# Fewer steps per layer norm, another division of the last tile's attention units, and a later shared expert in a two-layer decoder kernel

## The chip, the core and the metric

The kernel runs on one core of a Trainium2 chip. The core has a matrix engine (TensorE, PE in the profile, with its weight loads as PEld), a vector engine (VectorE, DVE), a scalar and activation engine (ScalarE, ACT), a general engine (GpSimd, POOL) that here mostly issues indirect DMAs, and a queue engine (SyncE, SP) that issues the other DMAs. Each engine works through its own list of instructions in order; semaphores make one wait for another. The metric is device time in microseconds from the start of the program to its end, lower is better; of several runs the median counts.

## The reference

Two decoder layers work on 4 sequences of 256 tokens, 256 wide. Cut to what is computed:

```python
x = x + linear_attention(layernorm(x))   # 16 heads, decayed running sums of k*v and k
x = x + experts_by_token_id(layernorm(x))  # 4 experts, weights taken from ctx
x = x + product_key_memory(layernorm(x)) # 8 heads, 8 of 45*45 rows each, gathered from a table
x = x + local_attention(layernorm(x))    # causal convolution, then blocks of 16 tokens
x = x + cross_attention(layernorm(x), ctx)  # 16 heads of 16, each token against 1024 keys
x = x + moe(layernorm(x))                # shared SwiGLU + 2 of 16 routed SwiGLU experts

def layernorm(x, eps=1e-05):
    m, v = mean(x), var(x)
    return (x - m) / sqrt(v + eps)
```

In the cross attention queries, keys and values are rounded to 8-bit steps, and so are the softmax weights: each row is scaled so that its largest entry is 255 and rounded to whole numbers. The last block is `shared_output + routed_output`, with the two gates divided by their sum.

## The kernel before

**Tiles.** The 1024 tokens lie in NT = 8 tiles of 128 rows; `xt[t]` is tile t's residual in SBUF. A batch is two tiles. The first three blocks run by batch in `front(b)`, the others by tile.

**Order.** TensorE, ScalarE and VectorE get their instructions in an order that the kernel makes itself. Every piece of work is a Python generator that yields the engine it needs next and, if it has to, a condition. `Clock` keeps an estimate of when each engine is free (`note`), and `weave` always advances the generator that could begin first, less its `lead`, then by `rank`. The estimates exist only while the program is built; what remains is a fixed order on each engine. So an instruction more or less in one generator can move all others after it. `fork` starts several generators and waits for them all. PSUM is given out in banks (`Banks.take`, `give`); from `turn` on there are two pairs and three single ones.

**Stages.** `front(b)` norms, projects with w_qkv, scans, norms, runs the four experts, norms, raises with w_up, lowers with w_down, projects with w_q, compares with keys, and `choose` finds the best rows on VectorE; its result is `idxT`. `fetches` then has POOL gather the rows: 64 chunks of eight indirect DMAs, three buffers `g`, so that a chunk is fetched only when the third before it was summed. `weigh` multiplies and reduces a chunk on VectorE (`g`, `z`, `u`), takes tanh on ScalarE, fills `blk` and sums on TensorE into `accs`. When tile t has all eight chunks, `local_attention(t)` and `queries(t)` follow, then 16 `units`, one per head.

**A unit** takes a pair of banks, makes scores for 1024 keys on TensorE (`psc`), their maximum on VectorE (`mx`), a bias from it on ScalarE (`nb`), the exponentials as uint8 on ScalarE (`e`), four bytes at a time transposed on TensorE, cast from uint8 to bf16 on ScalarE (`qqT`), and multiplied by the values on TensorE into `accs[:, 1]`. At most two units may be between transposition and sum. Three streams share all 128 units: stream k takes units k, k + 3 and so on.

**After the units.** `cross_out` divides, projects and adds. `routes` runs `route` for tiles (0,1), (2,3), (4,5), (6), (7): norm (its rows are stored to `xs` in DRAM), gate logits, two best experts, counts in `took` and `prior`, ranks. After tile 7 it forks `maps` (slots for all rows: `rmap` and `smap`), `gates` and `shared`; for the other tiles `gates` and `shared` follow one another. `shared` is the shared expert: `ph` from w_s13, tanh, `hd`, transposition, `py` from w_s2a and w_s2b, addition to `xt`. The expert loop (`up`, `down`, from line 1344) is outside `weave`: POOL gathers 128 rows by `smap`, TensorE transposes them (`tpx`), multiplies by the expert's weights, and POOL scatters the results by `rmap`. Its PSUM pool takes over the banks.

**The layer norm** computes a reciprocal root on VectorE, without a table: a first guess from the bits of the variance, then three Newton steps of three instructions each on a [128, n] tile (`layernorm_T`, from line 329).

Of the kernel before, what the change touches and what calls it, by code (L numbers as in the profile page):

```python
# [11 lines left out]
F32 = mybir.dt.float32  # L12
BF16 = mybir.dt.bfloat16
I32 = mybir.dt.int32
# [7 lines left out]
P = 128  # L22
# [182 lines left out]
def decoder(ctx, tc, a, out):  # L205
# [123 lines left out]
    def layernorm_T(pool, sfx, tiles, dst, col0=0, store=None):  # L329

        n = len(tiles)
        mv = pool.tile([P, n, 2], F32, name="ln_mv", tag="ln_mv" + sfx)
        for i, t in enumerate(tiles):
            st = pool.tile([P, 6], F32, name="ln_st", tag="ln_st" + sfx, bufs=2)
            ve_.bn_stats(st, xt[t])
            yield "vector", None
            ve_.bn_aggr(mv[:, i, :], st)
            yield "vector", None

        ve = pool.tile([P, n], F32, name="ln_ve", tag="ln_ve" + sfx)  # L340
        ve_.tensor_scalar(ve, mv[:, :, 1], EPS, None, ALU.add)
        yield "vector", None
        half = pool.tile([P, n], I32, name="ln_half", tag="ln_half" + sfx)
        ve_.tensor_scalar(half, ve.bitcast(I32), 1, None, ALU.logical_shift_right)
        yield "vector", None
        rstd = pool.tile([P, n], F32, name="ln_rstd", tag="ln_rstd" + sfx)
        ve_.tensor_scalar(rstd.bitcast(I32), half, -1.0, float(0x5F3759DF), ALU.mult, ALU.add)
        yield "vector", None
        nt = pool.tile([P, n], F32, name="ln_nt", tag="ln_nt" + sfx)
        for _ in range(3):  # L350
            ve_.scalar_tensor_tensor(nt, rstd, -0.5, rstd, ALU.mult, ALU.mult)
            yield "vector", None
            ve_.tensor_tensor(nt, nt, ve, ALU.mult)
            yield "vector", None
            ve_.scalar_tensor_tensor(rstd, nt, 1.5, rstd, ALU.add, ALU.mult)
            yield "vector", None
        nmr = pool.tile([P, n], F32, name="ln_nmr", tag="ln_nmr" + sfx)
        ve_.scalar_tensor_tensor(nmr, mv[:, :, 0], -1.0, rstd, ALU.mult, ALU.mult)
        yield "scalar", None
        xns = []  # L360
        for i, t in enumerate(tiles):
            xn = pool.tile([P, D], F32, name="ln_xn", tag="xnTq" if sfx == "q" else "ln_xn" + sfx,
                           bufs=1 if sfx in "lq" else 2)
            se_.activation(xn, xt[t], AF.Identity, scale=rstd[:, i:i + 1], bias=nmr[:, i:i + 1])
# [12 lines left out]
        yield "vector", None  # L377
# [673 lines left out]

    weighted = [0]

    def units(k, n):

        work = A.work
        for j in range(k, NT * XH, n):
            t, h = j // XH, j % XH
            yield "tensor", lambda: qready.get(t)
            o, c = h % 2, h // 2  # L1060
            hr = slice(o * 64, o * 64 + 64)
            psc = yield from bank.take([P, T], n=2)
            for n_ in range(2):
                te_.matmul(psc[:, n_ * 512:(n_ + 1) * 512], QT[t][hr, c, :], kT[hr, c, n_ * 512:(n_ + 1) * 512],
                           start=True, stop=True)
            yield "vector", None
            mx = work.tile([P, 1], F32, name="mx", tag="mx", bufs=4)
            ve_.tensor_reduce(mx, psc, AX.X, ALU.max)
            yield "scalar", None
            nb = work.tile([P, 1], F32, name="nb", tag="nb", bufs=4)  # L1070
            se_.activation(nb, mx, AF.Identity, scale=NSQ[t][:, h:h + 1], bias=ln255)

            e = work.tile([P, T], U8, name="e", tag="e", bufs=3)
            se_.activation(e, psc, AF.Exp, bias=nb, scale=SQ[t][:, h:h + 1], accum_out=SUMS[t][:, h:h + 1])
# [68 lines left out]
    def route(*tiles):  # L1143
        work = A.work2
        n, t0 = len(tiles), tiles[0]
        xnT = work.tile([P, 2, n * P], F32, name="xnT6", tag="xnT6")
        yield from layernorm_T(work, "r", tiles, xnT, store=xs)
        pl = yield from bank.take([P, n, NE])
        for i in range(n):
# [25 lines left out]
        se_.copy(rank[:, t0:t0 + n, :], prk)  # L1175
        bank.give(prk)
        if t0 + n == NT:
            yield from ck.fork(maps(), gates(tiles, sg), shared(tiles, xnT), ahead=(4.0, 0.0, 0.0))
        else:
            yield from gates(tiles, sg)  # L1180
            yield from shared(tiles, xnT)

    def gates(tiles, sg):
        work, n, t0 = A.work2, len(tiles), tiles[0]
# [7 lines left out]
        ve_.reciprocal(ws, ws)  # L1192
        ve_.tensor_tensor(gs, gs, ws.to_broadcast([P, n, 2]), ALU.mult)

    def shared(tiles, xnT):
        work, n = A.work2, len(tiles)
        yield "tensor", None

        hds = []
        for i, t in enumerate(tiles):  # L1200
            ph = yield from bank.take([P, 2, EI])
            for k in range(2):
                te_.matmul(ph.rearrange("p j n -> p (j n)"), xnT[:, k, i * P:(i + 1) * P], A.s13[:, k, :],
                           start=(k == 0), stop=(k == 1))
            yield "scalar", None
# [26 lines left out]
        bank.give(py)  # L1232
        yield "vector", None

    def maps():

        work, keep = A.work2, A.w2
        yield "tensor", None
        pcn = yield from bank.take([P, NE])
        te_.matmul(pcn, ones, prior[:, NT, :], start=True, stop=True)  # L1240
# [32 lines left out]
        for t0 in (0, NT):  # L1273
# [11 lines left out]
        ve_.tensor_tensor(past, bc(iotat, 2, NE), bc(last, 1, NSL), ALU.is_ge)  # L1285
        tef = work.tile([P, NSL], F32, name="tef", tag="tef")
        ve_.tensor_reduce(tef, past, AX.X, ALU.add)
        A.te = keep.tile([P, NSL], I32, name="te", tag="te")
        ve_.tensor_scalar(A.te, tef, float(NE - 1), None, ALU.min)
# [6 lines left out]
        bank.give(pmap)  # L1296
        A.smap = keep.tile([P, NSL], I32, name="smap", tag="smap")
        ve_.tensor_scalar(A.smap, A.rmap, 1, T - 1, ALU.logical_shift_right, ALU.bitwise_and)

        se_.activation(part0[:, 0:1], part0[:, 0:1], AF.Silu)  # L1300
        none = work.tile([P, NSL], F32, name="none", tag="none")
# [25 lines left out]
    with tc.manual_schedule(engines={mybir.EngineType.PE, mybir.EngineType.Activation, mybir.EngineType.DVE}):  # L1327

        ck.weave([*[Stream(follow(b), (3.0, 0.0, 0.0, 0.0)[b], (0.0, 20.0, 0.0, 0.0)[b], (0, 0, 1, 1)[b]) for b in range(NB)],
                  Stream(keys_values(), 0.0, 25.0, 1), Stream(fetches(), 20.0), Stream(weigh(), rank=0), Stream(turn()), Stream(free()),  # L1330
                  Stream(weights()), Stream(locals_()), Stream(all_queries(), rank=0), *[Stream(after_turn(units, k, 3)) for k in range(3)],
                  Stream(cross_out()), Stream(routes())])
    w13, w2a, w2b = A.w13, A.w2a, A.w2b
    work_ctx.close()
# [142 lines left out]
```

## Time and profile before

| what | value |
|---|---|
| runs | 1258.58, 1258.76, 1255.35 us; median 1258.58 |
| the profiled execution | 1113.02 us |
| its span, first to last instruction | 1111.3 us |
| mean granted TensorE clock in it | 0.752 of full speed |
| batch 0's front, up to the first gather | 0 to 111.7 us |
| gathers on POOL | 111.7 to 845.9 us, 512 of them |
| copy of tile 7's queries (qT) done | 929.6 us |
| last sum of tile 7's units | 982.0 us |
| first gather of the expert loop | 1004.7 us |
| first transposition of the expert loop | 1010.5 us |

The profiled execution took 1.7 us more than its span. It was 145.6 us shorter than the median of the runs. The profile is of one execution; its instruction times are those of that execution. A row of the timeline gives start, duration, engine, line, operation, output and inputs, shape and number of instructions merged, and in brackets how long the engine had been idle and who released it. Line 77 is the helper through which all woven instructions are recorded, so they are told apart by the names of their tiles.

### The profile page before, as it was taken

Reading aid. Unit: us, or ns where it says so; the run is one execution under the profiler, and the core shown is the slowest. Engines: PE = TensorE matmul, PEld = TensorE weight load, DVE = VectorE, ACT = ScalarE, POOL = GpSimd, SP = SyncE. Lnnn points to the kernel's source line nnn. Section 1 sums busy time; section 2 is a strip of 40 time slices with the busy share of each in tenths; the row PEclk is TensorE's granted clock in tenths of the full one; section 3 lists DMA queues with packets and bytes.
Section 4 is the critical chain, followed back from the end, with each engine's and each line's share of the span. In section 5 each row is a group of like instructions: output and inputs, shape, how many; then the busy total and the mean of one; then the engine's idle time right before and its main releaser. Section 6 shows DMA issues by size and latency. Waiting matters only on the chain. (4 is left out here: it accounts for less than half of the span.)

```text
span 1111.3 us, 15428 instructions
## 1 busy us (share of the span) xinstructions
PE 803.7 (72%) x4945; PEld 494.9 (45%) x4945; DVE 785.0 (71%) x2312; ACT 560.9 (50%) x1168; POOL 572.4 (52%) x597
## 2 busy tenths in 40 slices
PE   4772578926862887766887888878887777838993
PEld 3561455613650665333544554344543443314551
DVE  5459877688779768997778777788867676543233
ACT  2231232511421254655787767787767798832221
POOL 3000766575777577767777667776663000003551
PEclk9786678966985898665868686588956777556997
DMA  6001565586677578759876667767662600001223
GB/s 226 1 4 40 145 196 152 154 246 163 188 194 194 150 198 233 201 165 270 231 205 185 180 176 193 192 188 199 173 192 86 208 11 1 5 5 50 79 81 133
DMA packets 65710, 163.75 MB, mean 147 GB/s; under 512 B 14890, under 2 KB 28571, under 8 KB 65628
## 3 DMA queue, kind: packets, MB, share of 16 engines
q0 software_dynamic: 35072, 106.99, 33.9%
q1 hardware_dynamic: 29404, 54.18, 18.2%
q10 hardware_dynamic: 1152, 1.57, 0.4%
q8 instruction: 40, 0.66, 0.2%
q14 instruction: 42, 0.34, 0.1%
HBM read 156.93 MB, written 5.77 MB: 146 GB/s over the span
## 5 line engine op out<-in xcount | busy, mean ns | idle before, releaser
L77 POOL DMA_INDIRECT g<-in_table,idxT x512 | 517.2, 1010 | 319.4 <-issue 147.0
L77 DVE TENSOR_REDUCE mx<-bank 128x1 f32<-128x1024 f32 x128 | 155.1, 1217 | 60.7 <-PE bank L77 54.2
L77 ACT ACTIVATE e<-bank,nb,qs_q 128x1024 uint8<-128x1024 f32 x128 | 154.0, 1203 | 4.3
L77 PE MATMUL accs<-g,blk 128*32 128x256 f32 x1024 | 99.2, 523 | 71.4 <-DVE blk L77 64.6
L77 ACT CAST qqT<-bank 128x1024 bf16<-128x1024 uint8 x128 | 126.8, 1009 | 21.6 <-PE bank L77 20.8
L1349 POOL DMA_INDIRECT xr<-xs,smap x24 | 23.3, 969 | 183.0 <-DVE none L77 158.8
L77 PE MATMUL bank<-kT,qT 64*128 64x512 bf16 x256 | 98.3, 496 | 21.6 <-ACT e L77 19.6
L77 DVE TENSOR_TENSOR g<-g,hb 128x1024 f32<-128x1024 f32 x64 | 78.1, 1221 | 14.7 <-DMA g<-in_table,idxT 10.1
L77 PE MATMUL bank<-ident,e 128*128 128x128 f32 x256 | 68.2, 371 | 26.0 <-ACT e L77 19.5
L77 PEld LDWEIGHTS accs<-g,blk 128*32 128x32 f32 x1024 | 33.0, 136 | 119.2 <-DVE blk L77 76.9
L77 DVE TENSOR_REDUCE z<-g 128x8 f32<-128x1024 f32 x64 | 78.1, 1220 | 2.2
L77 ACT ACTIVATE nb<-mx,ln,nsq 128x1 f32<-128x1 f32 x128 | 49.6, 388 | 44.6 <-DVE mx L77 44.4
L77 PEld LDWEIGHTS <-qqT 128*128 128x128 bf16 x1024 | 38.4, 102 | 68.5 <-ACT qqT L77 49.2
L77 PEld LDWEIGHTS bank<-ident,e 128*128 128x128 f32 x256 | 34.1, 177 | 77.6 <-ACT e L77 35.1
L77 PE MATMUL accs<-vi,qqT 128*128 128x16 bf16 x1024 | 46.8, 174 | 22.4 <-ACT qqT L77 22.1
L77 ACT ACTIVATE th<-u 128x16 f32<-128x16 f32 x64 | 13.9, 218 | 96.1 <-DVE u L77 90.0
L77 ACT ACTIVATE ln_xn<-x,ln_nmr,ln_rstd 128x256 f32<-128x256 f32 x48 | 27.2, 595 | 39.4 <-DVE ln_nmr L77 37.9
L77 PE MATMUL bank<-ident,ln_xn 128*128 128x128 f32 x96 | 23.3, 354 | 32.6 <-ACT ln_xn L77 17.7
L1358 PE MATMUL ph<-w,xrT 128*128 x96 | 37.6, 512 | 5.0 <-DVE xrT L1355 5.0
L1362 DVE TENSOR_TENSOR hd<-hd,ph 128x176 f32<-128x176 f32 x24 | 8.1, 338 | 43.8 <-ACT hd L1361 43.8
L77 PE MATMUL bank<-w_ctxT,aT 128*128 128x256 f32 x128 | 32.8, 407 | 3.9 <-DVE aT L77 2.6
L77 PE MATMUL bank<-ident,ix 128*128 128x128 f32 x8 | 3.5, 439 | 42.8 <-DVE ix L77 42.8
(293 smaller groups left out, 1673.1 us busy)
## 6 DMA issues: line engine op xcount, KB each, us to landing
hb<-hdram SPq DMA_DIRECT2D x128, 256.0 KB
g<-in_table,idxT POOLq DMA_INDIRECT x512
w<-in_w SPq DMA_DIRECT2D x16, 352.0 KB
w_w2a<-in_w SPq DMA_DIRECT2D x1, 2048.0 KB
x<-in_x SPq DMA_DIRECT2D x8, 128.0 KB
w_ctxT<-in_ctxT SPq DMA_DIRECT2D x1, 1024.0 KB
w_w_up<-in_w_up SPq DMA_DIRECT2D x1, 1024.0 KB
xs<-ln_xn SPq DMA_DIRECT2D x8, 128.0 KB
```

What stands on the lines that cost most here:

```text
L77: return emit(*args, **kw)
L1349: nc.gpsimd.indirect_dma_start(out=xr, out_offset=None, in_=xs, in_offset=bass.IndirectOffsetOnAxis(ap=smap[:, i:i + 1], axis=0))
L1358: nc.tensor.matmul(ph.rearrange("p j n -> p (j n)"), xrT[:, k, :], w13[:, bass.ds(e, 1), k, :], start=(k == 0), stop=(k == 1))
L1362: nc.vector.tensor_tensor(hd, hd, ph[:, 1, :], ALU.mult)
```

## The change

It has four parts.

1. *Layer norm.* The three Newton steps become one third-order step (four instructions) and one Newton step (three), with a constant factor moved between them.
2. *Last tile's units.* `units` gets a range. Tiles 0 to 6 keep three streams, tile 7 has four of its own. For tile 7 `nb` is made by VectorE for all heads, and `qqT` by VectorE for odd heads.
3. *Shared experts.* Tile 6's `shared` no longer follows its `gates`: it becomes a stream of its own with a lead 2.0 smaller, which starts when tile 7's units are summed. Tile 7's waits for it, but its first product `ph`, and the counts `pcn` of `maps`, are put on TensorE before the fork. Tile 6 and tile 7 get their own `xnT6` buffers (the tag names tile 6 apart from the rest).
4. *Maps.* `rmap` and `smap` are computed before `past`, `tef` and `te` instead of after them; `past` takes the buffer of `cols`.

```diff
@@ layernorm_T
-        for _ in range(3):
-            ve_.scalar_tensor_tensor(nt, rstd, -0.5, rstd, ALU.mult, ALU.mult)
-            yield "vector", None
-            ve_.tensor_tensor(nt, nt, ve, ALU.mult)
-            yield "vector", None
-            ve_.scalar_tensor_tensor(rstd, nt, 1.5, rstd, ALU.add, ALU.mult)
-            yield "vector", None
+        ve_.tensor_tensor(nt, rstd, rstd, ALU.mult)
+        yield "vector", None
+        ve_.tensor_tensor(nt, nt, ve, ALU.mult)
+        yield "vector", None
+        ve_.scalar_tensor_tensor(nt, nt, -10.0 / 3.0, nt, ALU.add, ALU.mult)
+        yield "vector", None
+        ve_.scalar_tensor_tensor(rstd, nt, 5.0, rstd, ALU.add, ALU.mult)
+        yield "vector", None
+        ve_.scalar_tensor_tensor(nt, rstd, -0.5 * 0.375 ** 3, rstd, ALU.mult, ALU.mult)
+        yield "vector", None
+        ve_.tensor_tensor(nt, nt, ve, ALU.mult)
+        yield "vector", None
+        ve_.scalar_tensor_tensor(rstd, nt, 1.5 * 0.375, rstd, ALU.add, ALU.mult)
+        yield "vector", None
@@ units
-    def units(k, n):
+    def units(lo, hi, k, n):
-        for j in range(k, NT * XH, n):
+        for j in range(lo + k, hi, n):
...
-            yield "scalar", None
             nb = work.tile([P, 1], F32, name="nb", tag="nb", bufs=4)
-            se_.activation(nb, mx, AF.Identity, scale=NSQ[t][:, h:h + 1], bias=ln255)
+            if t < NT - 1:
+                yield "scalar", None
+                se_.activation(nb, mx, AF.Identity, scale=NSQ[t][:, h:h + 1], bias=ln255)
+            else:
+                ve_.tensor_scalar(nb, mx, NSQ[t][:, h:h + 1], ln255, ALU.mult, ALU.add)
+                yield "scalar", None
...
-            yield "scalar", None
+            late = t == NT - 1 and h % 2 == 1
+            yield "vector" if late else "scalar", None
             qqT = work.tile([P, 8, P], BF16, name="qqT", tag="qqT", bufs=2)
-            se_.copy(qqT.rearrange("p (o j) q -> p o j q", o=2), tp.bitcast(U8).rearrange("p o (q j) -> p o j q", j=4))
+            (ve_.tensor_copy if late else se_.copy)(qqT.rearrange("p (o j) q -> p o j q", o=2),
+                                                    tp.bitcast(U8).rearrange("p o (q j) -> p o j q", j=4))
@@ route
-        xnT = work.tile([P, 2, n * P], F32, name="xnT6", tag="xnT6")
+        xnT = work.tile([P, 2, n * P], F32, name="xnT6", tag=f"xnT6{t0 == NT - 2}")
...
         if t0 + n == NT:
-            yield from ck.fork(maps(), gates(tiles, sg), shared(tiles, xnT), ahead=(4.0, 0.0, 0.0))
+            yield "tensor", None
+            pcn = yield from bank.take([P, NE])
+            te_.matmul(pcn, ones, prior[:, NT, :], start=True, stop=True)
+            ph = yield from bank.take([P, 2, EI])
+            for k in range(2):
+                te_.matmul(ph.rearrange("p j n -> p (j n)"), xnT[:, k, :], A.s13[:, k, :], start=(k == 0), stop=(k == 1))
+            yield from ck.fork(maps(pcn), gates(tiles, sg), shared(tiles, xnT, ph), ahead=(4.0, 0.0, 0.0))
         else:
             yield from gates(tiles, sg)
-            yield from shared(tiles, xnT)
+            if t0 + n < NT - 1:
+                yield from shared(tiles, xnT)
+            else:
+                A.late = Stream(shared(tiles, xnT), ck.lead - 2.0, ck.end + ck.HOP, ck.rank)
+                ck.live.append(A.late)
@@ shared
-    def shared(tiles, xnT):
+    def shared(tiles, xnT, made=None):
-        yield "tensor", None
+        yield "scalar" if made else "tensor", lambda: summed.get(("x", NT - 1)) if tiles[-1] == NT - 2 else A.late.done if made else 0.0
...
@@ maps
         yield "vector", None
-        past = work.tile([P, NSL, NE], F32, name="past", tag="past")
...
         yield "scalar", None
         part0 = work.tile([P, NSL], F32, name="part0", tag="part0")
         se_.copy(part0, pmap[:, 0, :])
...
         ve_.tensor_scalar(A.smap, A.rmap, 1, T - 1, ALU.logical_shift_right, ALU.bitwise_and)
+        past = work.tile([P, NSL, NE], F32, name="past", tag="cols")
...
@@ weave
...
-                  *[Stream(after_turn(units, k, 3)) for k in range(3)],
+                  *[Stream(after_turn(units, 0, NT * XH - XH, k, 3)) for k in range(3)],
+                  *[Stream(after_turn(units, NT * XH - XH, NT * XH, k, 4)) for k in range(4)],
```

More of the change, by code (lines that the diff above doesn't have):

```diff
@@ L1193, in gates @@
         ve_.tensor_tensor(gs, gs, ws.to_broadcast([P, n, 2]), ALU.mult)
-    def shared(tiles, xnT):
+    def shared(tiles, xnT, made=None):
         work, n = A.work2, len(tiles)
-        yield "tensor", None
+        yield "scalar" if made else "tensor", lambda: summed.get(("x", NT - 1)) if tiles[-1] == NT - 2 else A.late.done if made else 0.0
         hds = []
         for i, t in enumerate(tiles):
[L1201 to L1205, printed above, removed]
+            ph = made
+            if ph is None:
+                ph = yield from bank.take([P, 2, EI])
+                for k in range(2):
+                    te_.matmul(ph.rearrange("p j n -> p (j n)"), xnT[:, k, i * P:(i + 1) * P], A.s13[:, k, :],
+                               start=(k == 0), stop=(k == 1))
+                yield "scalar", None
             th = work.tile([P, EI], F32, name="th6", tag="th6", bufs=1)
@@ L1233, in shared, with maps @@
         yield "vector", None
-    def maps():
+    def maps(pcn):
         work, keep = A.work2, A.w2
-        yield "tensor", None
-        pcn = yield from bank.take([P, NE])
-        te_.matmul(pcn, ones, prior[:, NT, :], start=True, stop=True)
         yield "vector", None
@@ L1283, in maps @@
             yield "vector", None
-        past = work.tile([P, NSL, NE], F32, name="past", tag="past")
[L1285 to L1289, printed above, removed]
         yield "scalar", None
@@ L1298, in maps @@
         ve_.tensor_scalar(A.smap, A.rmap, 1, T - 1, ALU.logical_shift_right, ALU.bitwise_and)
+        past = work.tile([P, NSL, NE], F32, name="past", tag="cols")
+        ve_.tensor_tensor(past, bc(iotat, 2, NE), bc(last, 1, NSL), ALU.is_ge)
+        tef = work.tile([P, NSL], F32, name="tef", tag="tef")
+        ve_.tensor_reduce(tef, past, AX.X, ALU.add)
+        A.te = keep.tile([P, NSL], I32, name="te", tag="te")
+        ve_.tensor_scalar(A.te, tef, float(NE - 1), None, ALU.min)
         se_.activation(part0[:, 0:1], part0[:, 0:1], AF.Silu)
@@ L1330, in decoder @@
                   Stream(keys_values(), 0.0, 25.0, 1), Stream(fetches(), 20.0), Stream(weigh(), rank=0), Stream(turn()), Stream(free()),
-                  Stream(weights()), Stream(locals_()), Stream(all_queries(), rank=0), *[Stream(after_turn(units, k, 3)) for k in range(3)],
+                  Stream(weights()), Stream(locals_()), Stream(all_queries(), rank=0), *[Stream(after_turn(units, 0, NT * XH - XH, k, 3)) for k in range(3)],
+                  *[Stream(after_turn(units, NT * XH - XH, NT * XH, k, 4)) for k in range(4)],
                   Stream(cross_out()), Stream(routes())])
```

## The prediction

> **What bounds the kernel now.** I read the page's engine shares first, then busy time by stage, then the waits.
>
> ```profile
> PE 803.7 (72%) x4945; PEld 494.9 (45%) x4945; DVE 785.0 (71%) x2312; ACT 560.9 (50%) x1168; POOL 572.4 (52%) x597
> ```
>
> No engine is full, so the shares alone say nothing: the stages differ. The stage cut (columns: stretch in us, its length, busy us of PE, PEld, DVE, ACT, POOL, granted PE clock, DMA share, GB/s) shows the last attention tile and the routing after it:
>
> ```profile
> 910.00:929.60 19.60, 15.78 (x102) 8.55 (x102) 13.19 (x41) 15.97 (x29) 0.00 (x0) 0.85 0.01 2
> 929.60:982.00 52.40, 38.87 (x224) 18.02 (x224) 26.81 (x54) 44.02 (x75) 0.00 (x0) 0.50 0.01 3
> 982.00:1004.70 22.70, 9.34 (x35) 5.61 (x35) 15.12 (x69) 3.62 (x9) 0.01 (x1) 0.50 0.02 7
> ```
>
> From 929.6 to 982 ScalarE is busy 44.0 of 52.4 us: it bounds tile 7's sixteen units. Before that, the waits show a long stage paced by the gathers:
>
> ```profile
> POOL g L77 <- ACT pT L77: 102.6, 1, 102.6
> ...
> POOL g L77 <- PE accs L77: 53.5, 24, 7.1
> ```
>
> The first gather starts at 111.7 us, once batch 0's front has delivered its indices; the last starts at 844.9. In between POOL issues 512 gathers at a pitch of 1.25 us (0.95 and a gap of 0.30), 640 us of the 734; 53.5 us more are waits for a chunk to be summed. So a late first gather is a late end, unless those waits shrink.
>
> **Seven operations for nine.** There are 33 layer norms (12 in fronts, 8 local, 8 query, 5 routing), so 66 VectorE instructions go, at a pitch of 0.195 us (36.13, 36.33, 36.52 in the timeline): 13 us of 785. Where the norm is on the path the gain is 0.39 us; elsewhere it only lightens an engine that is about 80% busy.
>
> *In batch 0's front* three norms are on the path: 1.2 us sooner. But the planner places by its own clock, and shorter norms move its choices. In the built order of the changed kernel, batch 1's norm transposes and its three projections (12 matmuls from w_qkv) stand on TensorE between batch 0's third norm and its projections from w_up. Before, w_up follows at once:
>
> ```profile
> 64.42 9.39 PE L77 MATMUL bank<-xnT,w_w_up 128*128 128x256 f32 x32 [0.73 <-ACT xnT L77]
> ...
> 68.24 0.84 ACT L77 ACTIVATE up<-bank,w_b_up 128x256 f32<-128x256 f32 x2 [3.87 <-PE bank L77]
> ```
>
> ```profile
> 64.40:68.30 3.90, 3.88 (x9) 3.17 (x10) 0.99 (x3) 0.06 (x1) 0.00 (x0) 0.50 0.00 0
> ```
>
> The first group of four matmuls takes 3.8 us because the clock is granted at 0.50 after the idle stretch; later groups take 1.8 (eight expert matmuls in 3.62). After the change the transposes end at about 62.5 instead of 63.7, the projections take 3.8 + 1.8 + 1.8 = 7.4, the first w_up group 1.8: ScalarE gets it at 71.7 instead of 68.2, 3.5 late. Batch 1's kf pair (1.2 us on ScalarE) is hidden, since ScalarE needs 1.5 per group and TensorE 1.8; its qf pair (1.2) falls between the qT copies, whose gaps of 0.28 hide 0.6. First gather: **+4** (range 0 to +8; the upper end if the clock stays at 0.50 for all three projections). Every later chunk queues behind it on POOL.
>
> *In the gather stage*, 24 norms (48 instructions, 9.4 us of VectorE) get shorter. POOL waits for summing in 53.5 of 734 us, 7%, so 0.7 is recovered; bounds 9.4 gained and 15 lost, the loss because the new interleaving may also make chunks wait: **-1**. POOL keeps its order, save that the iota issued by the free step comes 16 gathers sooner; SP moves some hdram stores with the fronts, and hb loads queue behind a store that waits for its htok copy. At the last chunk 96 units have been issued on TensorE instead of 97, at tile 7's query copy 112 in both: the stretch from the last gather to tile 7's queries keeps its work and gains its norms, **-1**.
>
> **Tile 7's units.** ScalarE loses sixteen nb (pitch 0.41) and eight qqT (0.9 each): 6.6 + 7.2, and tile 6's shared expert leaves (th and hT, 1): 44.0 to about 29. VectorE takes sixteen nb at 0.2 and eight qqT. The trace has no uint8 cast from PSUM on VectorE; the rows that bear on it:
>
> ```profile
> L77 DVE TENSOR_REDUCE mx<-bank 128x1 f32<-128x1024 f32 x128 | 155.1, 1217 | 60.7 <-PE bank L77 54.2 <-ACT qT L77 2.3 <-ACT qqT L77 1.8
> ...
> L1355 DVE COPY xrT<-tpx 128x256 f32<-128x256 f32 x24 | 9.7, 418 | 11.8 <-PE tpx L1353 11.8
> ...
> L77 DVE TENSOR_SCALAR v<-v,rv 128x1024 f32<-128x1024 f32 x2 | 1.5, 753 | 0.1
> ```
>
> A one-source pass over 1024 elements costs 0.75 from SBUF, a pass reading PSUM 1.22. Which is near? The Trainium skill, "VectorE: DVE Perf Modes", section "Mode 2×_2P — use both ports for one tensor", speaks against the move: the mode that reads one tensor through both ports needs SBUF, as PSUM has one read port. The PSUM copy at 0.418 for 256, above the 0.294 of a TENSOR_SCALAR on 256 in SBUF, fits it. By the SBUF row eight casts cost 6.0, by the rule and the PSUM rows 9.8; I take 9.8, and 14 as the bad end if the strided bytes cost more. VectorE then holds 26.8 - 1.1 (shared) - 0.4 (norm) + 3.2 + 9.8 = 38.3 and is the next bound. If it is as well filled as ScalarE was (84%), the stretch takes 45.5: **-7** (at 95% 40, so -12; with casts at 14, 50.5, -2).
>
> TensorE holds 38.9 here, 5.7 of it tile 6's shared expert (2.69 + 0.69 + 2.3), so 33.2 remain, below VectorE. "TensorE: Matmul & The Clock Gate", Part 1, says that a sustained busy window of about 3.4 us gives full rate; the row above has 74% busy and a clock of 0.50 throughout, so the row decides. At full rate 33 would be some 20, but it is not what bounds. Four streams instead of three bring no third score buffer: two bank pairs remain, one held about 4.4 us per unit (scores at 949.80, the next at 954.17), 2.2 per unit for two, 35 in all.
>
> **Past the last unit.** The norm gives 0.4. Tile 6's shared expert fills holes: its 2.69 us of up-projection stands while VectorE adds and normalises (985.8 to 989.4), its down-projection (2.4) and tile 7's up-projection (2.69) while VectorE computes the maps (994.5 to 1000.2), 5.1 of 5.7. With less cover it would show in full. What starts the experts:
>
> ```profile
> 1002.71 2.69 PE L77 MATMUL bank<-w_s,xnT 128*128 128x352 f32 x4
> ...
> 1006.16 0.34 DVE L77 TENSOR_TENSOR hd<-hd,bank 128x176 f32<-128x176 f32 x1
> ...
> 1010.01 0.42 DVE L77 SCALAR_TENSOR_TENSOR x<-bank,x 128x256 f32<-128x256 f32 x1 [3.51 <-PE bank L77]
> ...
> 1010.49 1.11 PE L1353 MATMUL tpx<-ident,xr 128*128 128x128 f32 x4 [0.52 <-DVE x L77]
> ```
>
> The first tpx waits for tile 7's addition of the shared expert, not for its rows (gathered from 1004.7). Now smap comes 0.9 sooner, but past and tef (1.4 together), which used to run while pmap was finished, follow it and stand with gates and tile 6's addition (0.42) ahead of tile 7's hd. Counting from the end of pmap: rmap and smap to 1003.5, past, tef, te 1005.1, none, rmap, used 1005.6, gates 1006.6, addition 1007.0, hd 1007.8 instead of 1006.5. The 2.69 saved on TensorE is thus lost to VectorE: +1.4. With the norm: **+1** (range -2 to +3).
>
> **Sum.** 4 - 1 - 1 - 7 + 1 = -4: 1109.0 for the profiled execution's 1113.0. The runs shown have a median of 1258.6, 145 us more, and no view shows where these lie; I carry the difference over unchanged: 1254.6. If they come from a lower TensorE clock, the delay in the front is larger (12 matmuls at 0.95 are 11.4); if from slower gathers, it passes in full and the -7 stays.
>
> **Rivals.**
> - *Waits of POOL on accs grow.* The new interleaving lets chunk sums come late more often. For it: 24 such waits, up to 7.1 us, mean 2.2; a different order everywhere. Against: VectorE has 9.4 us less to do there. Two more waits make the change worth nothing; from four more (about +8) it is slower by over 0.3%. With six: 1254.6 + 13 = 1268.
> - *The last tile gains little.* VectorE's casts cost 14, and mx queues behind them: -2 instead of -7, so +1: 1260. For it: nothing in the trace measures the cast; against: ScalarE's 44 of 52 drop by a third.
> - *The order does not slip in front.* The gathers start on time and the tile gains 12: 1113 - 1.2 - 1 - 1 - 12 + 1, some 14 less: 1244.
> - That the change does not take effect is excluded: the built order shows nb and eight qqT on VectorE.
>
> **Numbers.** A measurement of this kernel tells 0.3% (3.8 us) from no change. Forecast, 1247 to 1258: chance 0.37, of which 0.27 is faster and 0.10 within the bound. Little gain, 1255 to 1262: 0.14, of which 0.10 within the bound. Waits grow, 1260 to 1275: 0.27; the front slips further at a low clock, with the same end: 0.04. No slip, 1238 to 1249: 0.18.  Together: faster 0.45, within 0.3% 0.20, slower 0.35. Range 1239 to 1270; the forecast's own is 1247 to 1258.
>
> **What would show it.** First gather at 114 to 117 us; the last about 730 us after the first; POOL's waits on accs near 53; from tile 7's query copy to its last accs about 45 us with VectorE busy some 38; the casts at 1.2 us; from the last unit to the first tpx 29.5 us instead of 28.5. A first gather at or before 111, waits on accs above 65, or a last-tile stretch of 50 or more would prove the matching step wrong.

## The result, and the profile after

| kernel | runs | median |
|---|---|---|
| before | 1258.58, 1258.76, 1255.35, 1257.52 us | 1258.05 us |
| after | 1270.19, 1275.71, 1269.78, 1277.18 us | 1272.95 us |

The change makes the kernel slower: ratio 1.0149, 95% interval 1.0100 to 1.0198. A second comparison on another chip (20 executions after, 39 before) gave 1.0063, interval 1.0027 to 1.0100. The forecast was 1254.6, and its range ended at 1270.

Two things are needed to read what follows. First, the chips differ (or the sessions, for each of the named chips was used in one only). A result names its chip: on chips 4 and 15 the kernel before takes about 1119 and 1115 us, on chips 9, 2 and 7 about 1277, 1260 and 1258. The profile of before, at 1113 us, is like those of the first kind (the fast kind below); the runs, and the profile after (1270.19 us, span 1268.5), are like the second (the slow kind). So these two profiles can't be subtracted from each other; below, kernels are compared on one chip. Second, medians take in every execution and ratios leave disturbed ones out (on chips 9 and 2 more than half of before's), so the two can differ by up to 0.9%, and no stage behind the first gather is timed by the traces of norm7_kept, before_late and before_b2, which are of such executions.

The profile after, page lines first (engine shares), then the stage cut (stretch, length, busy us of PE, PEld, DVE, ACT, POOL, granted clock, DMA share, GB/s), cut at the first gather, the last gather, tile 7's query copy, the last sum of its units, the first tpx, and the end:

```profile
PE 843.8 (67%) x4945; PEld 522.2 (41%) x4945; DVE 790.4 (62%) x2270; ACT 545.9 (43%) x1144; POOL 570.3 (45%) x597
```

```profile
0.00:116.50 116.50, 66.41 (x282) 52.94 (x282) 69.21 (x285) 30.24 (x60) 8.38 (x37) 0.81 0.20 65
116.50:998.90 882.40, 574.27 (x3595) 357.20 (x3596) 573.46 (x1592) 382.92 (x809) 514.20 (x512) 0.69 0.58 158
998.90:1094.20 95.30, 78.49 (x526) 45.59 (x525) 62.99 (x159) 76.66 (x146) 0.95 (x1) 0.69 0.22 72
1094.20:1138.60 44.40, 31.29 (x204) 14.16 (x204) 37.09 (x69) 29.11 (x46) 0.00 (x0) 0.55 0.01 4
1138.60:1167.60 29.00, 17.18 (x53) 9.49 (x51) 17.69 (x78) 4.98 (x15) 3.01 (x3) 0.56 0.06 19
```

The front, tile 7 and the tail are close to what was forecast. The waits of POOL are not (who waited for whom: us, times, longest):

```profile
POOL g L77 <- PE accs L77: 174.3, 35, 15.5
...
POOL g L77 <- ACT pT L77: 107.4, 1, 107.4
```

The front's timeline shows the slip as the prediction read it out of the order: the projections of batch 1 (their 12 matmuls from w_qkv are the 24 of the row, two records to a matmul) stand ahead of w_up, and ScalarE gets its first group at 72.92 instead of 68.24.

```profile
63.94 7.22 PE L77 MATMUL bank<-xnT,w_w_qkv 128*128 128x256 f32 x24
71.00 2.75 PE L77 MATMUL bank<-xnT,w_w_up 128*128 128x256 f32 x12
...
72.92 0.84 ACT L77 ACTIVATE up<-bank,w_b_up 128x256 f32<-128x256 f32 x2 [8.10 <-PE bank L77]
```

In tile 7's stretch the group view has the two operations whose price was open: the cast on VectorE, and nb there.

```profile
L77 DVE TENSOR_REDUCE mx<-bank 128x1 f32<-128x1024 f32 x16 | 19.5, 1220 | 3.8 <-PE bank L77 3.5 <-ACT e L77 0.3
L77 DVE CAST qqT<-bank 128x1024 bf16<-128x1024 uint8 x8 | 9.7, 1216 | 2.2 <-PE bank L77 2.2
L77 DVE TENSOR_SCALAR nb<-mx,nsq,ln 128x1 f32<-128x1 f32 x16 | 4.4, 273 | 0.6
```

And the start of the experts, where past and tef now follow smap, and tile 7's hd follows these:

```profile
1159.77 0.67 DVE L77 TENSOR_TENSOR past<-iotat,last 128x496 f32<-128x496 f32 x1
...
1163.25 0.34 DVE L77 TENSOR_TENSOR hd<-hd,bank 128x176 f32<-128x176 f32 x1
...
1167.15 0.42 DVE L77 SCALAR_TENSOR_TENSOR x<-bank,x 128x256 f32<-128x256 f32 x1 [3.57 <-PE bank L77]
...
1167.63 1.11 PE L1380 MATMUL tpx<-ident,xr 128*128 128x128 f32 x4 [0.52 <-DVE x L77]
```

### The profile page after: what moved, and what is told of

Its sections match the earlier page's. It is cut to its first block, busy times and chain, and to the rows that moved or that the text cites. A ratio compares the mean times of both kernels' runs of the same rounds, so it can differ in the third digit from the quotient of the medians.

```text
span 1268.5 us, 15388 instructions
## 1 busy us (share of the span) xinstructions
PE 843.8 (67%) x4945; PEld 522.2 (41%) x4945; DVE 790.4 (62%) x2270; ACT 545.9 (43%) x1144; POOL 570.3 (45%) x597
## 4 chain that ended last, share of the span: by engine, by line
PE 37%; DVE 22%; ACT 11%; another core or an unknown queue 7%; issue 6%; DMA 3%; POOL 1%; DVEq 0%; SPq 0%; ACTq 0%; POOLq 0%
PE bank L77 26%; PE accs L77 6%; DVE mx L77 4%; ACT e L77 4%; ACT qqT L77 3%; DVE z L77 2%; DVE g L77 2%; PE ph L1385 2%; DMA g<-in_table,idxT 1%; DVE mi L77 1%; DVE oh L77 1%; DVE pk L77 1%; PE py L1402 1%; ACT nb L77 1%
## 5 line engine op out<-in xcount | busy, mean ns | idle before, releaser
L77 PE MATMUL accs<-g,blk 128*32 128x256 f32 x1024 | 105.2, 540 | 90.9 <-DVE blk L77 73.2
L77 ACT CAST qqT<-bank 128x1024 bf16<-128x1024 uint8 x120 | 119.9, 1009 | 72.9 <-PE bank L77 33.4
L77 PE MATMUL bank<-kT,qT 64*128 64x512 bf16 x256 | 107.1, 530 | 29.6 <-ACT e L77 20.0
L77 PE MATMUL bank<-ident,e 128*128 128x128 f32 x256 | 73.7, 387 | 32.7 <-ACT e L77 22.7
L77 ACT ACTIVATE nb<-mx,ln,nsq 128x1 f32<-128x1 f32 x112 | 43.4, 387 | 32.9 <-DVE mx L77 30.6
L77 PEld LDWEIGHTS <-qT 64*128 64x128 bf16 x256 | 17.3, 101 | 47.1 <-issue 41.1
```

The lines of the kernel that those rows point to most:

```text
L77: return emit(*args, **kw)
```

## The experiments

**Operations or order?** *norm7* is the kernel before with the seven operations alone. *norm7_kept* has them too, but the planner is told of nine, so that TensorE, ScalarE, POOL and SP have exactly the order of before:

```diff
+        for _ in range(2):
+            ck.note("vector", "scalar_tensor_tensor", rstd, (rstd, nt, 1.5, rstd), {})
+            yield "vector", None
```

*order9* is the reverse: the nine operations of before, the last two issued past the planner (through `nc.vector`, without their yields), which gives these engines norm7's order but for one weight load on SP. *before_again* is before, unchanged.

> The kernel before, unchanged, profiled once more. Theory 'unlike execution' (the 1113 us execution of the first profile ran without the pauses of the timed ones): this one takes about 1258 us, the first gather still starts near 112 us, POOL's waits on accs are 150 us or more instead of 53.5, and the stretch from the last gather to the end is again about 266 us. Theory 'the changed kernel alone has the pauses': it takes about 1113 us again, with waits on accs near 54.

> Only the layer norm's seven operations; last tile, shared experts and maps as before. The instruction order is the re-planned one. Theory 'order' (the new order, not the operations, costs the time): 1268 to 1285 us, first gather near 116. Theory 'tail' (the division of the last tile and the later shared expert lose): 1250 to 1259 us.

> The seven operations with the planner still counting nine, so that every engine has its instructions in the order of before, less 66 on VectorE. Theory 'order': 1252 to 1258 us, first gather near 110.5. Theory 'operations' (the shorter norm itself makes it slower, by whatever way): 1265 us or more.

> The nine operations of before, with the planner counting only seven: TensorE, ScalarE and POOL have their instructions in the order of norm7, VectorE does the arithmetic of before. Theory 'order': 1131 to 1137 us, as norm7 or slightly above. Theory 'operations' (new kinds of instructions in the norm cost the time): 1117 to 1123 us.

| run | chip | median, before beside it | ratio (95%) |
|---|---|---|---|
| before_again | 4 | 1118.84, 1119.29 | 1.0016 (0.9983 to 1.0048) |
| norm7 | 4 | 1132.77, 1119.29 | 1.0134 (1.0071 to 1.0197) |
| norm7_kept | 4 | 1119.20, 1119.29 | 1.0006 (0.9975 to 1.0037) |
| order9 | 9 | 1285.61, 1277.46 | 1.0152 (1.0108 to 1.0195) |

before_again came out as its second theory had it, but not for the reason given: later runs show the pauses in the order of before as well, on other chips. Neither theory said that chips differ. So the times in us that were expected of a run on the other kind of chip can't be met, and the ratios are compared. The shorter arithmetic in the old order (norm7_kept) changes nothing that can be measured. In the new order it loses on chip 4 (norm7), and the old arithmetic in the new order loses on chip 9 (order9: 1.0152, by the medians 1.0064), where the change itself lost 1.0063 (after_again, below). The 66 instructions saved are worth nothing that can be measured; the order they lead to costs some 0.6 to 1.5%.

Where norm7 loses it on chip 4 is read by cutting both at their own events. The kernel before (before_again):

```profile
111.70:845.00 733.30, 550.43 (x3678) 342.15 (x3682) 584.56 (x1653) 393.79 (x825) 516.89 (x513) 0.75 0.69 190
845.00:933.50 88.50, 70.39 (x460) 41.33 (x452) 57.90 (x152) 68.71 (x132) 0.93 (x1) 0.69 0.24 78
933.50:985.70 52.20, 38.86 (x224) 17.99 (x224) 26.81 (x54) 43.86 (x74) 0.00 (x0) 0.50 0.01 3
```

norm7:

```profile
116.50:857.30 740.80, 536.30 (x3601) 340.21 (x3602) 570.75 (x1593) 382.97 (x810) 522.44 (x512) 0.74 0.70 188
857.30:951.00 93.70, 76.46 (x521) 44.77 (x519) 62.74 (x158) 76.06 (x144) 0.95 (x1) 0.70 0.23 74
951.00:1003.80 52.80, 38.47 (x214) 16.67 (x214) 25.32 (x48) 43.05 (x73) 0.00 (x0) 0.53 0.01 3
```

The start is 4.8 us late, the gathers take 7.5 longer (740.8 - 733.3), and from the last gather to tile 7's queries 5.2 more (93.7 - 88.5); the rest is -0.4. That makes 17.1 between these two executions, 13.5 between the medians. In the gather stage all engines but POOL did *less* in norm7 and took longer over it: the same cut for ScalarE's qqT alone counts 90 units cast before the last gather in before, and 88 in norm7.

```profile
111.70:845.00 733.30, 89.14 (x90) 0.75 0.69 190
845.00:933.50 88.50, 21.04 (x22) 0.69 0.24 78
```

```profile
116.50:857.30 740.80, 87.66 (x88) 0.74 0.70 188
857.30:951.00 93.70, 24.09 (x25) 0.70 0.23 74
```

A unit costs ScalarE 2.79 us (e 1.205, its sum 0.19, nb 0.388, qqT 1.01), and two units left over are 5.6, near the 5.2 lost. The trace of after has 87 before its last gather, after_again 86.

Of the 7.5 of the stage only 1.5 are put down to waits for sums on this chip, as POOL's row of gathers shows for before_again and for norm7:

```profile
L77 POOL DMA_INDIRECT g<-in_table,idxT x512 | 517.7, 1011 | 319.0 <-issue 146.5 <-ACT pT L77 102.6 <-PE accs L77 54.7
```

```profile
L77 POOL DMA_INDIRECT g<-in_table,idxT x512 | 523.2, 1022 | 323.1 <-issue 136.9 <-ACT pT L77 107.4 <-PE accs L77 56.2
```

The gathers themselves took 5.5 longer; their idle time less the wait for pT is 215.7 against 216.4; and the moved iota has a gap of 2.8 before it. Together 7.6. The 2.8 are in effect a wait for a sum too: the gather behind the iota has to wait on for one.

```profile
428.25 0.97 POOL L77 DMA_INDIRECT g<-in_table,idxT  x1 [1.86 <-PE accs L77]
```

The 5.5 come from gathers that begin while VectorE multiplies `g` by `hb`; the last section shows that these take longer. About as many began there in both runs (61 and 62), but 37 of them took over 1.1 us in before_again and 49 in norm7. That this belongs to the order is not shown: late_double and norm7_kept, both in the old order, have 519.3 and 524.0 us of gathers, and norm7_b2, in the new order, 517.8.

**The other parts alone.** *rest* is the change with the nine operations put back, *after_kept* the whole change with the planner told of nine (the first diff above), *kept_b2* the same again.

> The last tile's units, the shared experts and the maps as in the change, with the nine operations of before; the order up to the last tiles is nearly that of before. Theory 'order': 1250 to 1256 us, first gather near 112, the last tile 45 us instead of 52. Theory 'tail': 1268 us or more, with the last tile at 55 us or more.

> The whole change with the planner counting nine operations per norm: the order of the kernel before up to the last tiles. Theory 'order' of either kind: ratio 0.993 to 1.001, the gain of the last tile less 1 or 2 us behind it; anything above 1.005 would say that a part other than the order costs time.

> The whole change in the order of before (planner counting nine): ratio 0.994 to 1.000 if the parts other than the order gain or cost nothing, on either kind of chip; above 1.005 if they lose. Tile 7's stretch 48 to 49 us against 52.2 in before.

| run | chip | median, before beside it | ratio (95%) |
|---|---|---|---|
| rest | 4 | 1118.22, 1119.29 | 0.9988 (0.9961 to 1.0014) |
| after_kept | 2 | 1264.80, 1260.37 | 1.0107 (1.0029 to 1.0185) |
| kept_b2 | 7 | 1260.72, 1258.20 | 0.9968 (0.9923 to 1.0014) |

By its ratio after_kept contradicts kept_b2, the same kernel; it ran four times, kept_b2 twelve. By the medians they are 1.0035 and 1.0020, and its profiled execution (span 1257.2) doesn't look like a loss either, so the 1.0107 is not built on. rest and kept_b2 say that the tail's edits neither lose nor clearly gain: both have 48.7 us from query copy to last sum, where in the old order one unit of tile 6 (a ninth qqT on ScalarE) still lies. In the new order it is 44.4 to 44.9. rest thus gains 3.5 there, too little to be told from no change. Its first gather came at 113.8, 2.1 later than in before_again, which no run explains.

**The change on another chip.** *after_again* is the changed kernel.

> The changed kernel, unchanged, profiled once more. If this chip runs the kernel before in about 1119 us: theory 'order' expects 1130 to 1136 us, that is the 13.5 us that the re-planned order cost without the other parts, less 1 to 3 for the last tile; without pauses in which TensorE, VectorE and ScalarE all stand still between first and last gather (none of over 1.5 us). Theory 'tail' (the parts together lose more than each alone): 1137 us or more. From tile 7's query copy to its last accs about 45 us in both.

On chip 9, of the slow kind, 1282.60 beside 1277.46, ratio 1.0063 (1.0027 to 1.0100). By the medians that is 1.0040. The first gather is at 116.6, tile 7 takes 44.9. The expectation was for a chip of the other kind, and the pauses are there again.

**The late start alone.** *before_late*, and *late_b2* again, is the kernel before with useless matmuls ahead of batch 0's first w_up group; *late_double* has 22 of them. No engine's order changes otherwise.

```diff
                 p = yield from bank.take([P, 2, N])
+                if b == 0 and g == 0:
+                    for i in range(10):
+                        nc.tensor.matmul(p[:, 0, :], w_up[:, 0, 0:P], xnT[:, 0, :], start=True, stop=True)
```

> The kernel before, every engine's order untouched, with ten useless matmuls (128x256, written over at once) ahead of batch 0's first w_up group on TensorE: the first gather should start near 116.5 us instead of 111.7, as in the changed kernel. Theory 'start' (a gather stage that starts 4.8 us later ends as much later, no more): ratio to before 1.003 to 1.006. Theory 'start, amplified' (the late start itself sets off further waits): 1.009 to 1.016. Theory 'later order' (the loss comes from the order after the fronts): 1.000 to 1.006.

> The kernel before with the ten useless matmuls ahead of batch 0's w_up again: first gather near 116.4 us, order of before. Theory 'start': 4 to 6 us slower than before (ratio 1.003 to 1.006) on either kind of chip. Theory 'backlog': the late start is worth at most 4.8 us on a chip of 1119 us and nothing on one of 1260 us, where the gather stage is not paced by the gathers; ratio 0.997 to 1.003 there, with as many units done at the last gather as in before.

> The kernel before in its own order with 22 useless matmuls ahead of batch 0's w_up, about twice the late start: first gather at 121 to 123 us, 10 us later than before. Theory 'start' (a late first gather is paid in full): ratio 1.007 to 1.010, on either kind of chip. Theory 'backlog' (what is lost is lost behind the start): on a chip of about 1260 us ratio 0.999 to 1.004, the first half of the gathers taking up most of the delay; on one of 1119 us up to 1.008.

| run | chip | first gather | median, before beside it | ratio (95%) |
|---|---|---|---|---|
| before_late | 2 | 116.4 | 1260.55, 1260.37 | 0.9983 (0.9934 to 1.0032) |
| late_b2 | 7 | 118.2 | 1274.24, 1258.20 | none (4 executions, 1256.03 to 1276.00) |
| late_double | 15 | 121.5 | 1125.03, 1115.35 | 1.0112 (1.0057 to 1.0168) |

On the fast kind of chip a start 9.8 us later (121.5 against 111.7 in before_again, on another chip of that kind) costs 9.7 by the medians: it is paid about in full. The ratio's interval, 6 to 19 us, doesn't exclude that something is added. On the slow kind a start some 4.7 us later cost nothing that can be measured in before_late (the interval ends at 4 us); late_b2 is inconclusive. So what the front's slip costs in the runs of the change, which were on the slow kind, is not settled.

**Which order?** *front_kept* has the seven operations, the planner told of nine for the norms of the fronts alone; *later_kept* the other way round. *n7_start26* and *after_start26* leave all counts at seven and let batch 1's stream start at 26.0 instead of 20.0 in the planner's clock, which also puts w_up ahead again; the first is the norm alone, the second the whole change. *after_front_kept* is the whole change in front_kept's manner:

```diff
+        if sfx not in ("l", "q", "r"):
+            for _ in range(2):
+                ck.note("vector", "scalar_tensor_tensor", rstd, (rstd, nt, 1.5, rstd), {})
+                yield "vector", None
```

> Norms of seven operations; the planner counts nine in the fronts and seven in the local attention, the queries and the routing. Batch 1's projections stay behind batch 0's w_up, so the first gather should be at 112 us or before. Theory 'front slip' (the late first gather carries the loss through the whole stage): 1117 to 1123 us. Theory 'interleaving' (the loss comes in the gather stage and at its end, from the order after the fronts): 1126 to 1134 us.

> The other way round: the planner counts seven operations in the fronts and nine in the later norms, so the first gather is late (near 116.5 us) and the later order changes only in answer to that. Theory 'front slip': 1123 us (only the 4.8 us of the first gather) to 1133 us. Theory 'interleaving': 1117 to 1124 us.

> Norms of seven operations, planner counting seven everywhere, batch 1's stream starting at 26 instead of 20 in the planner's clock: TensorE has batch 0's w_up ahead of batch 1's projections again, all later order is a third one, neither that of before nor that of the changed kernel. First gather at 110.5 to 112 us. Theory 'front slip': ratio 0.990 to 1.002. Theory 'later order' (any order but that of before loses): 1.006 to 1.015.

> The whole change with batch 1's stream starting at 26: first gather at 110.5 to 112 us, last tile 45 us from query copy to last accs. Theory 'front slip': ratio 0.985 to 0.999, faster than the change by 1 to 2%. Theory 'later order': 1.004 to 1.015.

> The whole change, the planner counting nine operations for the fronts' norms and seven for the others: batch 0's experts stay ahead of batch 1's projections, later order as in front_kept (more units done at the last gather than in before). Theory 'order' of either kind: ratio 0.984 to 0.996, faster than both kernels; last tile about 45 us. If it is above 1.003, front_kept's gain came by chance of its four executions, and an order alone does not explain the loss.

The table gives them with runs from above for comparison (order9 and after_again in the new order, after_kept and late_double in that of before): the time of the first gather, the length of the gather stage, POOL's waits on accs in it, the units cast before the last gather, and the time from there to the copy of tile 7's queries.

| run | chip | first | stage | on accs | units | to queries | median, before beside it | ratio (95%) |
|---|---|---|---|---|---|---|---|---|
| front_kept | 9 | 111.4 | 888.9 | 138.6 | 92 | 91.9 | 1274.66, 1277.46 | 0.9894 (0.9812 to 0.9975) |
| later_kept | 9 | 115.7 | 886.6 | 180.7 | 84 | 103.3 | 1298.30, 1277.46 | 1.0123 (1.0065 to 1.0182) |
| order9 | 9 | 116.2 | 888.5 | 167.2 | 86 | 98.7 | above | above |
| after_again | 9 | 116.6 | 892.0 | 183.6 | 86 | 97.5 | above | above |
| n7_start26 | 2 | 111.3 | 876.1 | 171.8 | 88 | 93.3 | 1258.42, 1260.37 | 1.0033 (0.9995 to 1.0071) |
| after_start26 | 2 | 112.2 | 870.9 | 168.4 | 88 | 93.3 | 1255.99, 1260.37 | 0.9979 (0.9925 to 1.0032) |
| after_kept | 2 | 110.8 | 876.9 | 130.4 | 90 | 91.7 | above | above |
| after_front_kept | 15 | 112.8 | 715.1 | 35.1 | 92 | 89.6 | 1098.26, 1115.35 | 0.9838 (0.9790 to 0.9887) |
| late_double | 15 | 121.5 | 735.2 | 54.5 | 90 | 86.5 | above | above |

after_front_kept beats before by far more than the edits by themselves: its slowest execution, 1105.45, lies below before's fastest, 1110.05. front_kept's gain is not sure, as its medians differ by 0.2% only. n7_start26 lies between its two theories, after_start26 where "front slip" had it, and after_front_kept just past its 0.984. later_kept loses 16 to 21 us, far more than its late start: its later order changed with it.

The late start and few units go with the losses. On the slow kind of chip the gather stage does not: on chip 9 it takes 887 to 892 us in all four orders, though the waits on accs are 139 to 184, and on chip 2 these waits are some 40 longer than in after_kept while the stage is no longer. What tells the orders on chip 9 apart is the start (111.4, or 115.7 to 116.6) and the stretch behind the last gather (91.9 with 92 units done, 97.5 to 103.3 with 84 to 86). For after_front_kept, the cut and POOL's row:

```profile
112.80:827.90 715.10, 532.37 (x3700) 333.04 (x3702) 582.47 (x1607) 397.38 (x834) 516.79 (x513) 0.77 0.71 195
827.90:917.50 89.60, 69.77 (x450) 41.73 (x442) 55.10 (x148) 63.91 (x124) 0.94 (x1) 0.65 0.23 77
917.50:962.30 44.80, 31.80 (x204) 14.62 (x204) 37.10 (x69) 29.09 (x46) 0.00 (x0) 0.54 0.01 3
```

```profile
L77 POOL DMA_INDIRECT g<-in_table,idxT x512 | 517.6, 1011 | 302.0 <-issue 142.9 <-ACT pT L77 103.7 <-PE accs L77 35.1
```

Against late_double, in the order of before on the same chip, the gather stage is 20.1 shorter (715.1 against 735.2), and the waits on accs are 19.4 shorter (35.1 against 54.5); against before_again, on another chip of this kind, it is 18.2 and 19.6. On the fast kind these waits are thus something that an order can change, here for the better. Tile 7 gives 7.4 more against before_again. The stretch after the last gather is no shorter (89.6 against 88.5), though two units fewer are left in it; so the count of units is not the whole of it.

**Before, norm7 and a late start on one chip.** *before_b2* is before, *norm7_b2* is norm7.

> The kernel before once more, for a profile on the same chip as the next three. On a chip on which it takes about 1119 us: no pause of over 1.5 us common to TensorE, VectorE and ScalarE between first and last gather, as in its first two profiles. On one on which it takes about 1260 us or more: theory 'pauses of the chip' expects over 40 us of such pauses in the kernel before, as in the changed one; theory 'pauses of the change' expects fewer than 10 us.

> Only the norm's seven operations, in the re-planned order, beside the kernel before on the same chip. Ratio 1.010 to 1.017 in both theories. Theory 'start' (what is lost is the late first gather): first gather 4.8 us later than in before, and no more than 3 us lost after it. Theory 'backlog' (fewer units are done when the gathers end): of the loss, 5 us or more lie between the last gather and the copy of tile 7's queries, with fewer units done at the last gather, on either kind of chip.

before_b2 took 1259.91 us on chip 7 (ratio 0.9965, 0.9930 to 1.0000), norm7_b2 1274.82 beside 1258.20: 1.0126 (1.0054 to 1.0198). norm7_b2 has 87 units before the last gather, before_b2 and kept_b2 90. Beside kept_b2, in the order of before, POOL's rows are, for kept_b2 and then for norm7_b2:

```profile
L77 POOL DMA_INDIRECT g<-in_table,idxT x512 | 517.0, 1010 | 463.8 <-issue 159.9 <-PE accs L77 134.5 <-ACT pT L77 102.4
```

```profile
L77 POOL DMA_INDIRECT g<-in_table,idxT x512 | 517.8, 1011 | 465.2 <-PE accs L77 179.1 <-issue 142.2 <-ACT pT L77 107.0
```

On this kind of chip the waits on accs do grow with the new order, by 44.6; but other idle time shrinks, and the stage from first to last gather is only 4.2 longer (881.8 against 877.6). That is no more than executions of the old order differ by: late_b2 has 883.1. The first gather is 4.6 later, the stretch after the last one 4.6 longer (95.9 against 91.3), so 13.4 up to tile 7's queries. The two expectations of norm7_b2 are thus each half met: 4.6 are the start, 4.6 the stretch behind the last gather (5 or more were expected of it), 4.2 lie between.

## Why the prediction was wrong, step by step

The step that failed is that the work behind the first gather would be what it was: -1 for the gather stage and -1 for the stretch to tile 7's queries were forecast. norm7 showed +7.5 and +5.2 on chip 4, norm7_b2 +4.2 and +4.6 on chip 7. For the second term the runs show what there was more to do; for the first the cause is open in the main.

- *First gather, +4: right.* 4.8 in after and in norm7. Its reason, twelve matmuls ahead of w_up, is in the timeline. One term of it did not come: the 1.2 us that three shorter norms were to give. The transposes of the third norm ended at 64.1, where 62.5 was forecast, and ScalarE's up came at 72.9 instead of 71.7.
- *Gather stage, -1, with bounds of 9.4 gained and 15 lost: missed, in part open.* It was priced by the waits of the old order (53.5 of 734 us) and by VectorE's lighter load, as if the new interleaving were as good as the old. An order can change this stage, from 735 to 715 us on chip 15. But of norm7's +7.5 on chip 4, 5.5 are longer gathers, which are not shown to be the order's, and the +4.2 on chip 7 is within what executions of the old order differ by.
- *Last gather to tile 7's queries, -1: failed.* The sentence was that this stretch "keeps its work and gains its norms". It had 2 to 3 units more to do. In the old order, with 90 units cast before the last gather, it takes 84.8 to 88.5 us on the fast kind of chip and 91.1 to 91.7 on the slow kind (seven traces); in norm7, order9 and the change, with 86 to 88 units, 93.7 and 95.3 to 98.7 (five). The number read from the built order, 96 units instead of 97 issued on TensorE ahead of the last chunk, pointed that way and was given no price; at 2.79 us of ScalarE a unit it had one.
- *Tile 7's units, -7: right* for the order that was built. 44.4 against the forecast 45.5, VectorE busy 37.1 (38.3 forecast), ScalarE 29.1 (29). In the old order the same edits gave 3.5. The cast takes 1.216, as the rows reading PSUM had it and as the Trainium skill's "VectorE: DVE Perf Modes", section "Mode 2×_2P — use both read ports for one tensor", let one expect, not 0.75; only nb was under-priced, 0.273 for 0.2.
- *Past the last unit, +1: right.* 29.0 from the last sum to tpx, against 28.5.
- *The 145 us carried over unchanged: right in use, wrong in kind.* They go with the chip. On such a chip POOL waits on accs for 134.5 us even in the old order, so the test "waits above 65" was set on the wrong scale.
- *Rivals.* "Waits of POOL on accs grow" (1268, chance 0.27) came near the number, but not by its mechanism. On the slow kind of chip the waits do grow, and the stage does not with them; on the fast kind norm7's hardly did (56.2, and the 2.8 before the iota), and the loss came all the same. "The order does not slip in front" is what after_front_kept makes true: forecast at 14 us less, it brought 17. That these are near is luck: tile 7 gave 7.4 of the 12 forecast, and the gather stage 18 to 20 where 1 was forecast.

With the two missed terms at what norm7 showed, the sum is 4 + 7.5 + 5.2 - 7 + 1 = +11, near the +14.9 of the first comparison and above the +5 to +8 of the second.

## What to carry to other kernels

Where a planner makes the order, an edit is two changes, and they can be priced and tried apart: keep the old order by telling the planner the old cost, or take the new order with the old work. If the built orders differ, count what stands ahead of each gate (units issued before the last chunk, matmuls ahead of the first gather) and price each such unit at its full time on the engine that is full after the gate (here ScalarE, and TensorE with it: each busy some 76 of norm7's 93.7 us). And before two profiles are subtracted, ask whether they come from one chip.

## What was not expected of the hardware

*The chips.* The slow kind shows stretches between first and last gather in which TensorE, VectorE and ScalarE all stand still for over 1.5 us: 58 us in after, 47 in norm7_b2, 45 in kept_b2 and 43 in late_b2, these two in the order of before. On chips 4 and 15 there are none. They go with the chip, or its session, and not with the change. They are less than half of the some 145 us between the two kinds, nearly all of which lie between first and last gather (877.6 us in kept_b2, 733.3 in before_again); the rest of these is open. This is one in the timeline of after; POOL goes on gathering through it:

```profile
135.64 1.03 PE L77 MATMUL bank<-identb,k 128*128 128x128 bf16 x8
...
143.52 1.01 ACT L77 COPY kT<-bank 128x1024 bf16<-128x1024 bf16 x1 [11.45 <-remote]
...
149.81 0.69 DVE L77 TENSOR_TENSOR kf<-kf,bank 128x512 f32<-128x512 f32 x1 [15.06 <-remote]
```

In norm7 on chip 4 the same kf came 1.11 us after its predecessor. What ended the pause the profile doesn't know ("remote"), and no run shows the cause.

*Gathers beside VectorE.* A gather takes 0.95 us on POOL, but up to 2.0 in places. In after, the first of these began during a pass of VectorE over two inputs in SBUF and ended 0.8 us after it; the second began during z, which has one input, and was not held up:

```profile
994.10 1.22 DVE L77 TENSOR_TENSOR g<-g,hb 128x1024 f32<-128x1024 f32 x1
994.38 1.75 POOL L77 DMA_INDIRECT g<-in_table,idxT  x1 [0.30 <-issue]
...
995.35 1.22 DVE L77 TENSOR_REDUCE z<-g 128x8 f32<-128x1024 f32 x1
...
996.43 0.95 POOL L77 DMA_INDIRECT g<-in_table,idxT  x1 [0.30 <-issue]
```

It is so over whole traces. In before_again 61 gathers began during such a pass (`g<-g,hb`), and 37 of them took over 1.1 us; of the 62 that began during z, the 82 during mx (which reads PSUM) and the 102 with VectorE idle, none did. In norm7 it is 49 of 62 and none of 60, 75 and 113. A gather that overlaps z and is long, as the first one above, had begun before z.

The Trainium skill's "GPSIMD Engine Reference", section "1. Specifications", says that the two share their SBUF interface and contend when VectorE reads two inputs there, which fits these counts. No run changed such passes to see the gathers change with them.
